# A transformer block's attention: where the score products stand among the four heads' transposed scores

## The chip, the cores and the metric

The kernel runs on one core of a Trainium2 chip. The metric is the time of one execution on the device in microseconds, as a median of several runs.

## What is computed

One transformer block with adaptive modulation, in fp32, on x of 2 batch rows x 2048 tokens x 512 channels, 16 heads of 32 channels, a hidden layer of 2048:

```python
mod = jax.nn.silu(condition) @ Wada + bada
sh_a, sc_a, gt_a, sh_m, sc_m, gt_m = jnp.split(mod, 6, axis=1)
xm = layernorm(x, g1, be1) * (1.0 + sc_a[:, None, :]) + sh_a[:, None, :]
x = x + gt_a[:, None, :] * attention(xm, Wqkv, Wproj, bproj)
xm = layernorm(x, g2, be2) * (1.0 + sc_m[:, None, :]) + sh_m[:, None, :]
h = gelu(xm @ W1 + b1)
return x + gt_m[:, None, :] * (h @ W2 + b2)
```

The attention is causal: scores q k^T * 32**-0.5, a softmax over the keys up to the query's own place, then times v.

## The kernel before

**Stages.** For each batch row: layer norm, modulation and the q, k, v products (class Qkv), then attention (attention_phase), then the output projection (project_phase). The feed-forward part follows for both rows at the end. q and k are split into a high and a low part of 32 channels each, which stand side by side, so that one product with 128 contraction rows gives a head's full score.

**Units and steps.** Attention of one row is cut into 16 units: four groups of four heads (c), each with four blocks of 512 queries (i), in the order of the list units. A unit goes through its keys in steps of one tile of 128 keys (steps_of, line 631), with the last three diagonal tiles in two steps. A step (scores_t, line 524) makes the *transposed scores* of the four heads, keys down and queries across: first four selector products (line 550: sel with fold) that put minus the query's maximum into each head's st bank, then for every head the product of keys and queries on top of it (line 558). ScalarE takes the exponential of each head's bank into a tile e (line 566); GpSimd masks it on the diagonal (line 572) and adds pairs of e (line 592). Two steps later (LAG) the value products (o from e and vv, line 606) and the row sums (sm) follow.

**Score products.** The maxima that a unit needs have to be known before its own steps begin. They come from plain scores, queries down and keys across: Row.bank (line 422) makes one product of up to 512 keys in a PSUM bank, and VectorE reduces it to a maximum (lines 436 and 441, mx). Row.split (line 444) makes the high and low part of a unit's maxima, Row.rows (line 492) spreads them into fold. These score products are put among the steps of the units ahead. How many a step gets is planned: every product has a cost (line 267), every step a weight and a due time (due, line 644), and row.count (line 460) gives n for the step. Row.score(n, borrow) (line 470) issues n products; each takes one of two s banks, or, where borrow is given, every other one a bank of the ring of four st banks. A step issues more than five before its selectors (line 545). Up to five remain: those of head h follow it if h >= HC - n (line 579), and a fifth comes at the end (line 581). The one behind head 2 is the *borrowed* score product.

**Banks.** PSUM has two s banks, four st banks, one o and one sm. The st ring is taken in order: four heads, then the borrowed product, which gets the bank that the step's head 0 had; the next step's four heads get those of heads 1, 2, 3 and the borrowed one. A bank is free when its reader, ScalarE's exponential or VectorE's reduction, is through.

**Order.** Matmuls, exponentials, masks and sums are kept in program order (mm, line 190, and act, line 194); an instruction that waits holds up those behind it on its engine. The last unit has no score products left.

Of the kernel before, what the change touches and what calls it, by code (L numbers as in the profile page):

```python
# [27 lines left out]
def dit_block_kernel(  # L28
# [41 lines left out]
    HC = P // HD  # L70
# [119 lines left out]
    def mm(*args, **kw):  # L190

        return tc.keep_in_program_order(nc.tensor.matmul(*args, **kw))  # L192

    def act(ins):

        return tc.keep_in_program_order(ins)
# [318 lines left out]
    def attention_phase(row):  # L515
        b, vv, kst, qst = row.b, row.vv, row.kst, row.qst
        with pool(f"att{b}") as ap, pool(
# [6 lines left out]
            def scores_t(u, step, n):  # L524

                def st_bank():

                    n_bank[0] += u == len(units) - 1
                    if n_bank[0] % 6 > HC:
                        return ps_sp.tile([P, QB], F32, tag="s", name="st")
                    return ps_stp.tile([P, QB], F32, tag="st", name="st")

                c, i = units[u]  # L540
                tiles = steps_of[u][step]
                q0 = tiles[0][1]
                w = sum(QB - q for _, q in tiles)
                sts, es = [], []
                row.score(max(0, n - 5))
                n = min(n, 5)
                for h in range(HC):
                    g = slice(h * HD, (h + 1) * HD)
                    st = st_bank()
                    mm(  # L550
                        st[:, :w], sel[g, :], fold[u % 2][g, q0 : q0 + w],
                        start=True, stop=False,
                    )
                    sts.append(st)
                for h in range(HC):
                    at = 0
                    for j, q in tiles:
                        mm(
                            sts[h][:, at : at + QB - q],
                            kst[c][:, h, j * P : (j + 1) * P],  # L560
                            qst[u][:, h, q:],
                            start=False, stop=at + QB - q == w,
                        )
                        at += QB - q
                    e = ap.tile([P, QB], F32, tag="e", name="e", bufs=E_BUFS)
                    act(nc.scalar.activation(e[:, :w], sts[h][:, :w], AF.Exp))  # L566
                    if tiles[0][0] >= i * TQ:

                        d = e.rearrange("p (t k) -> p t k", k=P)[:, 0 : TQ : TQ - 1, :]
                        d = d[:, : len(tiles), :]  # L570
                        act(
                            nc.gpsimd.affine_select(  # L572
                                d, d, pattern=[[0, len(tiles)], [1, P]],
                                compare_op=ALU.is_ge, fill=0.0,
                                base=0, channel_multiplier=-1,
                            )
                        )
                    es.append(e)
                    if h >= HC - n:
                        row.score(1, st_bank if h == 2 else None)  # L580
                row.score(n - HC)
                return es

            def new_sums():
# [59 lines left out]
            def due(u, step):  # L644

                rate, past = 0.0, weight[step]
                for v in range(u + 1, len(units)):

                    left = sum(weight[step : max(step + 1, starts[v] - 3)])
                    rate = max(rate, (cum[v] - row.spent) / left)  # L650
                return row.spent + rate * past

            for u, (c, i) in enumerate(units):
# [5 lines left out]
                for n_step, tiles in enumerate(steps_of[u]):  # L659
                    last = n_step == steps - 1  # L660
                    if n_step == 0:
# [4 lines left out]
                    n = row.count(  # L666
                        due(u, starts[u] + n_step) - QB // 2, u + AHEAD
                    )
                    es = scores_t(u, n_step, n)
                    make_rows = False  # L670
                    if u + 1 < len(units) and row.rows_made == u + 1:
# [300 lines left out]
    row = Row(0)  # L972
# [115 lines left out]
    first, row = row, Row(1)  # L1088
# [31 lines left out]
    with ExitStack() as mlp:  # L1120
# [249 lines left out]
        for m in range(NM):  # L1370
            h = [
                [
                    mp.tile([P, 4, MT], F32, tag="h4", name="h4", bufs=2 * FC // 4)
                    for _ in range(FC // 4)
                ]
                for _ in range(2)
            ]
# [87 lines left out]
```

## Time and profile before

| what | value |
|---|---|
| median of 3 runs | 2526.72 us (2524.92 to 2527.82) |
| profiled execution, its own time | 2526.39 us |
| its span in the profile | 2524.7 us |
| granted TensorE clock, mean | 0.99 |
| attention of row 0 | about 225 to 760 us of the span |
| attention of row 1 | about 1100 to 1653 us of the span |
| score products in all (s and borrowed) | 1058 + 222 |
| mean VectorE reduction of a 128x512 bank (L441) | 686 ns |
| mean exponential of one head (L566) | 576 ns |

Names: PE is TensorE's matmuls, PEld its weight loads, DVE VectorE, ACT ScalarE, POOL GpSimd, SPq SyncE's queue of transfers. A row of the timeline gives the start and the length in us, the engine, the line of the kernel, the operation, the tiles out<-in, the sizes, how many alike follow each other (x4), and in brackets the idle time before it and what ended that. A row of the groups view gives the same with a count, the busy time and the mean in ns, and the idle time ahead of the group with what ended most of it. A row of waits names an engine and tile, whom it waited for, total us, times and the longest. Nearly all matmuls carry line 192, that of a helper, so they are told apart by tiles: `s<-kst,qst` is a score product in an s bank, `st<-kst,qst` a borrowed one, `st<-qst,kst` a head's transposed scores, `st<-fold,sel` a selector product.

### The profile page before, as it was taken

To read this page: it belongs to the slowest core of one execution; us is meant where nothing else is said; L and a number is where in the kernel's file an instruction comes from. 1 tells how busy PE (TensorE), PEld (TensorE's weight loads), DVE (VectorE), ACT (ScalarE), POOL (GpSimd) and SP (SyncE) were. 2 spreads that over 40 slices of the span, in tenths; PEclk is the share of its full clock that TensorE was granted. 3 is DMA by queue.
4 is the path that set the end of the run, shared out by engine and by line. 5 is a ranking of instruction groups with operands and counts; after the bars stand their busy time and mean duration, and the time that the engine had idled before them with its cause. 6 is when DMAs were issued, how large, how long until landed. Compare 5 with 4: busy or idle time off the path is not lost.

```text
span 2524.7 us, 30931 instructions
## 1 busy us (share of the span) xinstructions
PE 2460.4 (97%) x10977; PEld 1172.8 (46%) x10977; DVE 1351.5 (54%) x2820; ACT 895.1 (35%) x1667; POOL 982.0 (39%) x1158
## 2 busy tenths in 40 slices
PE   7999999999999899999999999999999999999998
PEld 3445445444444344554444444444444444444443
DVE  3465657667565625656675756665353353344424
ACT  2213455454545011155545454613312312311310
POOL 0062786766772362058767785241101201200200
PEclk9999999999999999999999999999999999999999
DMA  6667123041224596450514113163223233322422
GB/s 221 208 223 193 39 52 84 22 109 43 87 90 141 193 296 200 133 109 22 109 43 93 39 38 134 68 219 119 87 92 132 85 100 108 108 93 72 140 84 96
DMA packets 133445, 285.71 MB, mean 113 GB/s; under 512 B 13301, under 2 KB 42525, under 8 KB 128426
## 3 DMA queue, kind: packets, MB, share of 16 engines
q1 hardware_dynamic: 126226, 257.47, 34.2%
q0 software_dynamic: 5376, 23.07, 2.6%
q10 hardware_dynamic: 1688, 3.19, 0.4%
q8 instruction: 86, 1.41, 0.2%
q14 instruction: 69, 0.57, 0.1%
HBM read 209.76 MB, written 81.79 MB: 115 GB/s over the span
## 4 chain that ended last, share of the span: by engine, by line
PE 61%; DVE 2%; DMA 1%; SPq 1%; issue 0%; ACT 0%; POOL 0%; DVEq 0%; ACTq 0%
PE ps_y L192 15%; PE ps_h L192 15%; PE st L192 9%; PE o L192 5%; PE s L192 4%; PE ps_qk L192 4%; PE ps_o L192 2%; PE sm L192 2%; PE ps_v L192 2%; SPq L336 1%; PE ps_xt L200 1%; DVE junk L436 1%; PE ps_o L200 0%; DVE mx L441 0%; DMA r<-sum 0%
## 5 line engine op out<-in xcount | busy, mean ns | idle before, releaser
L566 ACT ACTIVATE e<-st 128x512 f32<-128x512 f32 (+1 forms) x1152 | 575.3, 576 | 509.4 <-PE st L192 460.5
L441 DVE TENSOR_REDUCE mx<-s 128x1 f32<-128x512 f32 x616 | 413.7, 686 | 273.5 <-PE s L192 272.1
L592 POOL TENSOR_TENSOR ee<-e 128x512 f32<-128x512 f32 x336 | 420.9, 1287 | 246.3 <-ACT e L566 245.7
L192 PE MATMUL s<-kst,qst 128*128 128x512 f32 (+3 forms) x1058 | 453.5, 447 | 17.8 <-DVE mx L436 8.5
L192 PE MATMUL st<-qst,kst 128*128 128x512 f32 (+3 forms) x1280 | 438.1, 392 | 0.0
L192 PE MATMUL o<-e,vv 128*32 128x512 f32 (+3 forms) x2560 | 294.9, 542 | 0.0
L192 PE MATMUL ps_h<-sx,w 128*128 128x512 f32 x640 | 286.7, 592 | 0.0
L436 DVE CUSTOM_DVE_ANT_0 junk<-s,causal 128x384 bf16<-128x384 f32 (+3 forms) x442 | 211.1, 478 | 138.9 <-PE s L192 130.6
L1236 POOL TENSOR_TENSOR c<-c 128x512 f32<-128x512 f32 x32 | 40.6, 1270 | 620.9 <-DVE c L1198 620.9
L192 PE MATMUL ps_y<-sh,w 128*128 128x512 f32 x640 | 277.5, 593 | 0.0
L192 PEld LDWEIGHTS st<-qst,kst 128*128 128x128 f32 x1280 | 230.4, 192 | 88.0 <-issue 63.3
L192 PEld LDWEIGHTS s<-kst,qst 128*128 128x128 f32 x1058 | 199.3, 190 | 144.0 <-issue 47.7
L192 PE MATMUL ps_qk<-xmT,wqkv 128*128 128x512 f32 x512 | 242.3, 601 | 2.2 <-DVE xmT L248 2.2
L572 POOL TENSOR_SCALAR_AFFINE_SELECT e<-e 128x128 f32<-128x128 f32 (+1 forms) x384 | 124.3, 341 | 289.3 <-ACT e L566 282.8
L1198 DVE TENSOR_TENSOR h<-c,ps_h 128x512 f32<-128x512 f32 x128 | 88.0, 687 | 232.5 <-PE ps_h L192 232.5
L592 POOL TENSOR_TENSOR ee<-ee 128x512 f32<-128x512 f32 x168 | 210.8, 1283 | 0.0
L192 PEld LDWEIGHTS ps_h<-sx,w 128*128 128x128 f32 x640 | 121.1, 190 | 150.2 <-issue 149.5
L192 PEld LDWEIGHTS ps_y<-sh,w 128*128 128x128 f32 x640 | 121.1, 191 | 148.3 <-issue 146.9
L192 PE MATMUL st<-fold,sel 32*128 32x512 f32 (+1 forms) x1152 | 156.8, 485 | 2.7 <-DVE fold L500 2.0
L1222 ACT ACTIVATE h<-h,cols 128x512 f32<-128x512 f32 x128 | 92.3, 721 | 182.0 <-DVE h L1198 182.0
L192 PEld LDWEIGHTS st<-fold,sel 32*128 32x128 f32 x1152 | 62.2, 183 | 183.8 <-ACT e L566 124.8
L192 PEld LDWEIGHTS ps_qk<-xmT,wqkv 128*128 128x128 f32 x512 | 95.2, 192 | 98.9 <-issue 91.8
(124 smaller groups left out, 2368.9 us busy)
## 6 DMA issues: line engine op xcount, KB each, us to landing
qst<-q SPq DMA_DIRECT2D x128, 256.0 KB
w<-w1d SPq DMA_DIRECT2D x34, 896.0 KB
w<-w2d SPq DMA_DIRECT2D x28, 1024.0 KB
kst<-k SPq DMA_DIRECT2D x24, 1024.0 KB
q<-hl SPq DMA_DIRECT2D x32, 512.0 KB
k<-hl SPq DMA_DIRECT2D x32, 512.0 KB
kst<-k SPq DMA_DIRECT2D x32, 256.0 KB
w<-in_L_cond_W_dram POOLq DMA_DIRECT2D x64, 128.0 KB, 4.7
```

The costliest lines, as they stand in the source:

```text
L192: return tc.keep_in_program_order(nc.tensor.matmul(*args, **kw))
L200: return tc.keep_in_program_order(nc.tensor.transpose(dst, src, ident[:n, :n]))
L336: nc.sync.dma_start(dst, inv_d[self.b][u].unsqueeze(1).to_broadcast([HC, HD, QB]),)
L436: nc.vector.tensor_tensor_reduce(junk[:, :w], s[:, :w], causal[:, QB - w :], 1.0, MASKED, ALU.add, ALU.max, m,)
L441: nc.vector.tensor_reduce(m, s[:, :w], axis=AX.X, op=ALU.max)
L566: act(nc.scalar.activation(e[:, :w], sts[h][:, :w], AF.Exp))
L572: nc.gpsimd.affine_select(d, d, pattern=[[0, len(tiles)], [1, P]], compare_op=ALU.is_ge, fill=0.0, base=0, channel_multiplier=-1,)
L592: act(engine.tensor_tensor(dst, x, y, ALU.add))
L1198: nc.vector.tensor_tensor(dst, x, y, op)
L1222: nc.scalar.activation(d, d, AF.Gelu, bias=col(r_b1 + chunk, 1))
L1236: nc.gpsimd.tensor_tensor(c1_, c1_, c2_, ALU.subtract)
```

## The change

In a step with n of three or more score products (after the cap at five), one follows head 0 and one follows head 1, both in s banks; the third is borrowed and stands behind head 3; the others follow it, in s banks. In a step with fewer than three they stand as before, behind the last heads, and none is borrowed. The list of score products, their number in each step, the sizes and all other work are the same.

```diff
                     es.append(e)
-                    if h >= HC - n:
-                        row.score(1, st_bank if h == 2 else None)
-                row.score(n - HC)
+                    if h < 2 and n >= 3 or h >= HC - n and n < 3:
+                        row.score(1)
+                if n >= 3:
+                    row.score(1, st_bank)
+                    row.score(n - 3)
                 return es
```

## Prediction

> **What bounds the kernel now.** I read the page first, then the costliest groups, then the timeline of single steps. The page shows TensorE busy nearly throughout, so a gain has to be a hole between TensorE's products or an interval in which its next weights are not in.
>
> ```profile
> PE 2460.4 (97%) x10977; PEld 1172.8 (46%) x10977; DVE 1351.5 (54%) x2820; ACT 895.1 (35%) x1667; POOL 982.0 (39%) x1158
> ```
>
> The groups view says where TensorE's weight loads wait. The borrowed score products (tile st, but operands kst and qst exchanged) number 222, and their loads wait for ScalarE almost alone; the other score products wait for VectorE.
>
> ```profile
> L192 PEld LDWEIGHTS s<-kst,qst 128*128 128x128 f32 x1058 | 199.3, 190 | 144.0 <-issue 47.7 <-DVE mx L441 47.3 <-DVE mx L436 20.9
> L192 PEld LDWEIGHTS st<-kst,qst 128*128 128x128 f32 x222 | 41.8, 188 | 57.7 <-ACT e L566 56.0
> ```
>
> The timeline of a step with four score products shows what such a wait costs. First the weight loads, then the matmuls:
>
> ```profile
> 618.89 0.19 PEld L192 LDWEIGHTS st<-qst,kst 128*128 128x128 f32 x1
> 619.34 0.19 PEld L192 LDWEIGHTS st<-kst,qst 128*128 128x128 f32 x1 [0.26 <-ACT e L566]
> 619.45 0.19 PEld L192 LDWEIGHTS st<-qst,kst 128*128 128x128 f32 x1
> ```
> ```profile
> 619.12 0.40 PE L192 MATMUL st<-qst,kst 128*128 128x512 f32 x1
> 619.35 0.49 PE L192 MATMUL st<-kst,qst 128*128 128x512 f32 x1
> 619.68 0.39 PE L192 MATMUL st<-qst,kst 128*128 128x512 f32 x1
> 619.91 0.40 PE L192 MATMUL s<-kst,qst 128*128 128x512 f32 x1
> 621.23 0.50 PE L192 MATMUL st<-fold,sel 32*128 32x512 f32 x4
> ```
>
> 512-wide products follow each other in 0.23 us. The borrowed one holds its bank until ScalarE has finished the first head's exponential. Its load comes at 619.34 instead of 619.12, so it no longer lies under the product before it, and the next product starts 0.33 us later: 0.10 us lost. ScalarE's row gives the release: four exponentials from 618.69, each 576 ns, so the first ends at 619.27.
>
> ```profile
> 618.69 2.07 ACT L566 ACTIVATE e<-st 128x512 f32<-128x512 f32 x4 [0.43 <-PE st L192]
> ```
>
> With five score products the last of them can wait as well, for VectorE to read the second of the two s banks (0.34 us idle here):
>
> ```profile
> 630.20 0.19 PEld L192 LDWEIGHTS st<-kst,qst 128*128 128x128 f32 x1 [0.27 <-ACT e L566]
> ...
> 631.08 0.19 PEld L192 LDWEIGHTS s<-kst,qst 128*128 128x128 f32 x1 [0.34 <-DVE mx L441]
> ```
>
> With two, the borrowed product follows three heads directly and TensorE stands still:
>
> ```profile
> 648.64 0.96 PE L192 MATMUL st<-qst,kst 128*128 128x512 f32 x3
> 649.89 0.50 PE L192 MATMUL st<-kst,qst 128*128 128x512 f32 x1 [0.29 <-ACT e L566]
> ```
>
> [...] loads normally start with the product before (0.23 us apart), and a waiting borrowed product holds up the fourth head's product behind it. [...] I count distances between successive products, not idle time. [...] the 128x16 cast takes 0.17 us at best and up to 1.27 us between 500 and 760 us.
>
> **The change part by part.** *Which steps.* Working through the planner's costs and due times gives per batch row 54 steps with 5 products, 26 with 4, 23 with 6, 3 with 7, 4 with 2 and one with 3; doubled, 222, as in the groups. The timeline shows the same number in every step. Nothing of the counts, the order in which score products are taken, or other engines' work changes.
>
> *Four and more products (212 steps).* Order now: head 0, s, head 1, s, head 2, borrowed, head 3, s, s. After: head 0, s, head 1, s, head 2, head 3, borrowed, s, s. Only the borrowed product and head 3 change places. The borrowed one is due 0.23 us later, and waits for the same exponential. Its loss here was 0.08 to 0.25 us in nearly every step, larger where a narrow product ahead shortens the way, so the shift covers nearly all of it: bound 0 to (old loss less 0.23), I take 0. What is late next is the last score product: its s bank is free only when VectorE has read the product two before it, and that moment does not move. So I rebuilt the end of every step from the timeline: the borrowed product without loss, each last score product at the later of its own pace and (observed end of that reduction + 0.06 us to the load + 0.50 us to its end, narrower ones less).
>
> *Three (2 steps).* Both plain products go first, the borrowed one last: loss 0.33 each gone. *Two (8 steps).* No borrowing any more; both products use s banks, behind heads 2 and 3, that VectorE has long read. Loss 0.56 each gone; bound 0 to a VectorE wait of some 0.3 us, I take 0.
>
> Sums over both rows, in us (products in the step: steps, loss at the borrowed product, of it kept at the step's end):
> 2: 8, 4.5, 4.5. 3: 2, 0.7, 0.7. 4: 52, 6.2, 4.8. 5: 108, 15.8, 3.8. 6 and 7: 52, 7.2, 1.5. Together 34.4, of which 15.2 (before rounding) is kept; three steps that lie in a stretch of lowered clock are set at nothing kept. Of the 108 steps with five products, 78 keep nothing: their last score product waits for VectorE anyway.
>
> *To be taken off.* (a) After six of the eight two-product steps ScalarE is late: fourth exponential done 0.10 + 2.08 + 0.06 us after head 0's product, selector load wanted at 5 x 0.23 + 0.93 = 2.08 (0.93 from the end of the last score product, 620.30, to that load, 621.23, in the first step shown): 0.16 each, 1.0 together. (b) In the fourteenth unit VectorE waits for a load of the sums, which SyncE issues behind ten slow transfers:
>
> ```profile
> 689.77 20.54 SPq L336 DMA_DIRECT2D wide<-inv  x10
> 710.36 2.41 SPq L322 DMA_DIRECT2D r<-sum  x1
> ```
> ```profile
> 721.59 0.25 DVE L329 RECIPROCAL r<-r 128x16 f32<-128x16 f32 x1 [4.54 <-DMA r<-sum]
> ```
>
> What eight steps gain ahead of it is waited away: 0.45 per row, 0.9. (c) Steps that end sooner leave VectorE less time to catch up: bound 0 to 3, I take 0.5. The sum: 15.2 - 1.0 - 0.9 - 0.5 = 12.8 us.
>
> *New queue.* The borrowed product's wait now has the last one or two s products and the value products behind it instead of head 3. Head 3's product ends up to 0.43 us sooner, which gives ScalarE nothing: it is still at the earlier heads (four in 2.07 us). VectorE gets the borrowed product 0.03 (loss was 0.2) to 0.13 us later (loss was 0.1), while it is usually still on the second product. The next step's fourth selector product needs that bank: in the step above, read at 620.07 + 0.69 = 620.76, wanted at 621.23, so 0.4 us of slack.
>
> The profiled execution took 2526.4 us, the median is 2526.7. 2526.4 - 12.8 = **2513.6 us**.
>
> **Rivals.** (1) VectorE paces every step with four or more products: not only the waits seen but the slack elsewhere is used up. For it: VectorE waits of 47.3 + 20.9 us stand ahead of score loads. Against: in 40 of the 52 four-product steps no such wait follows. Left: 4.5 + 0.7 - 1.0 = 4.2, so 2522.2 us. (2) Slower: the borrowed product reaches VectorE 0.13 us later in the 89 steps whose loss was near 0.1, VectorE runs dry, and the delay reaches TensorE through the fourth head's bank or the next step's s bank. It decides once VectorE is 0.4 us later than shown. If two such delays a step stick, 2 x 89 x 0.13 = 23, less 4.2: 2545 us; half of it, 2534. Against: VectorE works without a gap from the second product into the borrowed one in the step shown. (3) More: collisions of VectorE with GpSimd at the splits fall otherwise. At 594 to 598 us one makes two score products wait 1.10 and 0.52 us; four such places, two per row: up to 6 us more, 2507.5.
>
> **How the numbers follow.** About 0.2% (5 us) is what a measurement of this kernel can tell from no change. Forecast as worked, 2508 to 2519: 0.75. Rival 1, 2519 to 2525: 0.13. Rival 2: 0.05. Rival 3, below 2508: 0.07. Faster: 0.75 + 0.07 + 0.01 of rival 1's lower part = 0.83; same 0.12; slower 0.05. The range, 2507 to 2520, takes in (c) at 0 and at 3, the first sum without any deduction (2511.2), a part of rivals 1 and 3, and leaves out less than 2 in 10.
>
> **What would show it.** In the changed kernel 214 borrowed products, and nearly none of the 56 us of waiting for ScalarE ahead of their loads; more than 68 us of waiting for VectorE ahead of s loads; four-product steps shorter by 0.1 to 0.2 us, wide five-product steps as long as before, the two-product steps before units' ends shorter by 0.5 us. It is wrong if borrowed loads still wait, if selector loads wait for VectorE, or if the four-product steps keep their length.

## The result, and the profile after

| | before | after |
|---|---|---|
| median, us | 2528.39 (2524.21 to 2530.41, 10 runs) | 2519.30 (2513.87 to 2529.32, 10 runs) |
| profiled execution, its own time | 2526.39 | 2519.99 |
| its span | 2524.7 | 2518.3 |

The ratio is 0.9967 (95% interval 0.9952 to 0.9982), a gain of 9.1 us by the medians where 12.8 was forecast; the interval allows 4.6 to 12.1. The forecast of 2513.6 us lies below every one of the runs, of which the best took 2513.87. The direction was right, the size was not.

The page and the groups view of the kernel after, in the same form as those shown of before:

```profile
PE 2445.9 (97%) x10977; PEld 1181.8 (47%) x10977; DVE 1412.4 (56%) x2820; ACT 891.6 (35%) x1667; POOL 981.3 (39%) x1158
```
```profile
L192 PEld LDWEIGHTS s<-kst,qst 128*128 128x128 f32 x1066 | 201.5, 189 | 168.6 <-DVE mx L441 68.1 <-issue 47.4 <-DVE mx L436 26.4
L192 PEld LDWEIGHTS st<-kst,qst 128*128 128x128 f32 x214 | 40.5, 189 | 16.1 <-ACT e L566 0.8
```

There are 214 borrowed products, and of 56.0 us of waiting for ScalarE 0.8 are left. The s loads wait 94.5 us for VectorE instead of 68.2. One number doesn't fit a change of order only: VectorE has the same 2820 instructions, but is busy for 1412.4 us instead of 1351.5.

The end of a step with four products, matmuls on the timeline:

```profile
613.77 0.63 PE L192 MATMUL st<-qst,kst 128*128 128x512 f32 x2
614.24 0.39 PE L192 MATMUL st<-kst,qst 128*128 128x512 f32 x1
614.47 0.40 PE L192 MATMUL s<-kst,qst 128*128 128x512 f32 x1
```

The heads' last two, the borrowed product and the s product follow each other in 0.23 us. In a step with five the wait has moved to the load of the last product:

```profile
625.48 0.19 PEld L192 LDWEIGHTS s<-kst,qst 128*128 128x128 f32 x1 [0.42 <-DVE mx L441]
```

And in a step with two, where 0.29 us of idle time stood before the product behind the third head, it follows at once:

```profile
642.70 0.96 PE L192 MATMUL st<-qst,kst 128*128 128x512 f32 x3
643.50 0.39 PE L192 MATMUL s<-kst,qst 128*128 128x512 f32 x1
```

**Where the rest went.** The time from each step's first head product to the next step's, called the step's length here, says where the loss is. Only three of the 288 steps are longer in the kernel after by more than 0.2 us, if those are left aside in which the clock fell (below): the first step of the ninth and thirteenth units of row 0 and of the fifth unit of row 1, by 1.86, 1.13 and 3.21 us, of the last 1.7 by the clock. A load in the first of them, in the kernel after:

```profile
512.58 0.19 PEld L192 LDWEIGHTS s<-kst,qst 128*128 128x128 f32 x1 [2.04 <-DVE mx L441]
```

VectorE reads that bank late since it was standing at the cast of Row.split (line 455), 128x16 elements. Such an instruction is called held below, and the time that it takes a hold:

```profile
497.00 14.68 DVE L455 CAST mhl<-m 128x16 fp32r<-128x16 f32 x1
...
511.85 0.68 DVE L441 TENSOR_REDUCE mx<-s 128x1 f32<-128x512 f32 x1
```

GpSimd works without a gap over these 14.7 us:

```profile
494.24 10.00 POOL L594 TENSOR_TENSOR ee<-e 128x512 f32<-128x512 f32 x8
504.14 1.10 POOL L572 TENSOR_SCALAR_AFFINE_SELECT e<-e 128x128 f32<-128x128 f32 x4
505.16 2.56 POOL L594 TENSOR_TENSOR ee<-ee 128x512 f32<-128x512 f32 x2
507.62 1.54 POOL L572 TENSOR_SCALAR_AFFINE_SELECT e<-e 128x256 f32<-128x256 f32 x4
509.07 2.57 POOL L594 TENSOR_TENSOR ee<-ee 128x512 f32<-128x512 f32 x2
```

The same place in the kernel before, VectorE and GpSimd:

```profile
503.70 1.27 DVE L455 CAST mhl<-m 128x16 fp32r<-128x16 f32 x1
```
```profile
499.93 5.01 POOL L592 TENSOR_TENSOR ee<-e 128x512 f32<-128x512 f32 x4
505.18 4.99 POOL L592 TENSOR_TENSOR ee<-e 128x512 f32<-128x512 f32 x4 [0.24 <-ACT e L566]
```

There GpSimd ran out of exponentials for 0.24 us at 504.94, and the cast ended at 504.97. In the kernel before all six splits of this kind, those of the sixth, tenth and fourteenth units of either row, end their cast within 0.04 us of the start of such a gap, of 0.24 to 0.71 us. After the change TensorE and ScalarE are further ahead at this place: the exponential that GpSimd had to wait for is done 0.7 us before GpSimd comes to it, and the gap is gone, here and at the other five. The tile view gives a cast's minimum, median and maximum in ns, first for after, then for before; with the subtractions (line 456, up to 6573 ns against 1210) the sum over both is 89.5 us against 30.3, which is 59.2 of the 60.9 us that VectorE is busier.

```profile
L455 DVE CAST mhl<-m x24: 164/776/14695, 166.8 to 1587.6; 128x16 fp32r<-128x16 f32 x24
```
```profile
L455 DVE CAST mhl<-m x24: 165/810/1270, 166.7 to 1594.6; 128x16 fp32r<-128x16 f32 x24
```

**The clock.** A second thing has to be taken out before steps are compared. In the fourteenth unit TensorE waits behind the load of the sums, in row 0 of the kernel after for 4.62 us without a product, and its granted clock falls to 0.50 for some microseconds, which is called a dip here. The stretches show it (columns: stretch, its length, busy time of PE, granted clock, DMA share, GB/s), again of the kernel after:

```profile
715.00:717.00 2.00, 0.00 (x0) 0.85 0.28 112
717.00:719.00 2.00, 1.70 (x6) 0.50 0.16 49
719.00:721.00 2.00, 2.00 (x8) 0.50 0.10 28
721.00:723.00 2.00, 2.00 (x14) 0.50 0.25 94
723.00:725.00 2.00, 2.00 (x12) 0.94 0.02 9
```

A stretch is counted as losing its length times (1 - clock). Eight value products show what it stands for: 1.94 us at 720.15, with the clock at 0.50, and 1.06 at 724.62, with 1.00. Here the loss is 2 x (0.15 + 0.50 + 0.50 + 0.50 + 0.06) = 3.4 us; at the same place of the kernel before, with clocks of 0.80, 0.50 and 0.85 in three such stretches, 2 x (0.20 + 0.50 + 0.15) = 1.7. All dips in the thirteen profiles of this study, but for those that the end of the span cuts off, cost close to 1.7 us, or two or three times as much; in the kernels before and after they last 3.41, 6.83 or 10.24 us at a clock of 0.50. They agree in place too: in each profile's record of the clock they start whole multiples of the shortest one's length apart (in the kernel before, those at 449.13 and 722.20 us, by 273.07 us, which is 80 times 3.413), and counted back from a dip to the start of the span, whole lengths leave another remainder in each (1.98 us in the kernel before, 3.02 in the one after). That one kernel's execution can gain or lose 1.7 or 3.4 us at a place without any cause in its code is inferred from this and not shown, since each kernel was profiled once. Below, a ledger is the sum of the differences of step lengths between two profiles, by the number of score products in the step. It has the clock's part taken out of every step, as the sum of (1 - clock) over half-microsecond stretches.

### The profile page after: what moved, and what is told of

It is laid out like the page before. It is cut to its first block, busy times and chain, and to the rows that moved or that the text cites. A ratio compares the mean times of both kernels' runs of the same rounds, so it can differ in the third digit from the quotient of the medians.

```text
span 2518.3 us, 30927 instructions
## 1 busy us (share of the span) xinstructions
PE 2445.9 (97%) x10977; PEld 1181.8 (47%) x10977; DVE 1412.4 (56%) x2820; ACT 891.6 (35%) x1667; POOL 981.3 (39%) x1158
## 4 chain that ended last, share of the span: by engine, by line
PE 86%; DVE 8%; DMA 3%; SPq 2%; issue 1%; ACT 1%; POOL 0%; DVEq 0%; ACTq 0%; POOLq 0%
PE st L192 16%; PE ps_y L192 15%; PE ps_h L192 15%; PE o L192 9%; PE ps_qk L192 8%; PE s L192 8%; PE sm L192 4%; PE ps_v L192 4%; PE ps_o L192 3%; DVE mx L441 2%; DVE mhl L455 2%; SPq L336 2%; DMA r<-sum 1%; DVE junk L436 1%; PE ps_xt L200 1%
## 5 line engine op out<-in xcount | busy, mean ns | idle before, releaser
L192 PE MATMUL s<-kst,qst 128*128 128x512 f32 (+3 forms) x1066 | 468.7, 454 | 29.3 <-DVE mx L441 15.4
L192 PE MATMUL st<-qst,kst 128*128 128x512 f32 (+3 forms) x1280 | 403.5, 391 | 0.0
L436 DVE CUSTOM_DVE_ANT_0 junk<-s,causal 128x256 bf16<-128x256 f32 (+3 forms) x444 | 211.9, 477 | 132.4 <-PE s L192 123.9
L192 PEld LDWEIGHTS st<-qst,kst 128*128 128x128 f32 x1280 | 224.2, 191 | 92.8 <-issue 63.2
```

The costliest lines, as they stand in the source:

```text
L436: nc.vector.tensor_tensor_reduce(junk[:, :w], s[:, :w], causal[:, QB - w :], 1.0, MASKED, ALU.add, ALU.max, m,)
```

## The experiments

Times are compared with runs of the kernel before on the same chip. After that comes what the ledger of the steps says.

### One part at a time

Only the part for three and more products:

```diff
-                    if h < 2 and n >= 3 or h >= HC - n and n < 3:
+                    if h < 2 and n >= 3:
                         row.score(1)
+                    elif h >= HC - n and n < 3:
+                        row.score(1, st_bank if h == 2 else None)
```

> Only the part of the change for three or more score products; steps with two borrow behind head 2 as before. Theory A (the missing gain is a hold: VectorE's 128x16 split of the maxima finds no gap in GpSimd's run of sums and masks, and first score products of units 5, 9 and 13 wait for it): the borrowed products keep their gain, some 10 us against the kernel before; whether the hold is there depends on whether GpSimd still has its 0.24 us gap near the end of units 4, 8 and 12. With gaps: casts of at most 1.3 us and 9 to 11 us faster than before; without: casts of 7 to 15 us and 3 to 5 us faster. Rival B (VectorE's reductions alone pace the steps, the casts cost nothing): 5 to 6 us faster than before whatever the casts take.

Measured: 2519.02 us (2515.53 to 2520.47, 5 runs) against 2527.09 (12 runs), ratio 0.9963 (0.9951 to 0.9976). Steps with four products gain 4.6 us over both rows, with five 4.3, with three 0.7. The long casts are there: 14.1 us in the tenth split of row 0 and the sixth of row 1, where the next unit's first step loses 1.1 and 1.4 us (in row 0 a dip of the clock adds 1.7), and 7.0 and 6.8 us at two others, where nothing is lost. In the last place of either row GpSimd still has a gap of 0.24 and 0.20 us, and the casts take 1.28 and 1.33.

Only the part for two products:

```diff
-                    if h < 2 and n >= 3 or h >= HC - n and n < 3:
-                        row.score(1)
-                if n >= 3:
-                    row.score(1, st_bank)
-                    row.score(n - 3)
+                    if h >= HC - n:
+                        row.score(1, st_bank if h == 2 and n >= 3 else None)
+                row.score(n - HC)
```

> Only the part for fewer than three: eight steps lose their borrowed product, all others as in the kernel before. Theory A: each of the eight steps is shorter by 0.41 to 0.56 us, 3.7 us in all, but in six of them the maxima of a unit are completed, so the split comes early into GpSimd's run: casts of several us appear, the first score products of units 5, 9 and 13 wait 1 to 3 us in some places, and the total is between 3.7 us faster and 3 us slower than before. Rival B: 3.7 us faster, no long cast.

Measured: 2523.01 us (2518.87 to 2530.82, 8 runs), ratio 0.9983 (0.9970 to 0.9997). The eight steps gain 3.7 us. No cast takes more than 1.39 us, so the expectation of long casts fell, and its rival B, 3.7 us and no long cast, came true. But that is not because GpSimd kept its gaps. At four of the six places it has none, and VectorE still gets in, with the cast at the end of one of GpSimd's additions (502.14 us here) and with the subtraction at the end of the next (503.39):

```profile
501.59 0.59 DVE L455 CAST mhl<-m 128x16 fp32r<-128x16 f32 x1
502.21 1.22 DVE L456 TENSOR_TENSOR mhl<-m,mhl 128x16 fp32r<-128x16 f32 x1
```
```profile
500.85 7.48 POOL L592 TENSOR_TENSOR ee<-e 128x512 f32<-128x512 f32 x6
```

So a gap always ended a hold, and a missing gap did not always make a long one. In the six profiles of this study that leave these splits, or their subtraction alone, on VectorE, ten of the 36 places have a gap, and their holds take at most 1.4 us; 26 have none, of which 22 hold VectorE for 6.8 us or more and these four for 1.8 us with both instructions. By the medians the two parts of the change gain 8.1 and 4.1 us by themselves, and only 9.1 together.

### The split away from VectorE

Both instructions of the split on GpSimd, in program order with its sums; once in the kernel after, once in the kernel before:

```diff
-            nc.vector.tensor_copy(hl[:, :, :, 0], m)
-            nc.vector.tensor_tensor(
-                hl[:, :, :, 1], m, hl[:, :, :, 0].bitcast(F32), ALU.subtract
-            )
+            act(nc.gpsimd.tensor_copy(hl[:, :, :, 0], m))
+            act(
+                nc.gpsimd.tensor_tensor(
+                    hl[:, :, :, 1], m, hl[:, :, :, 0].bitcast(F32), ALU.subtract
+                )
+            )
```

> The changed kernel with the two small operations of the split (128x16 cast and subtraction) on GpSimd instead of VectorE. Theory A: no VectorE instruction stands held, the 6.2 us of waits at the first steps of units 5, 9 and 13 go, and the four places in units 7 and 11 where two score products wait 1.0 and 0.5 us go too: 8 to 12 us faster than the changed kernel, 17 to 21 faster than the kernel before, and the runs lie closer together. Rival B: within 2 us of the changed kernel, since the reductions stay as they are. Rival C (GpSimd is itself the late engine): GpSimd's longer queue delays masks and sums, value products wait, 2 to 6 us slower than the changed kernel.

> The kernel before with the same two operations on GpSimd. Theory A: the holds of the kernel before are short (at most 1.3 us) and reach TensorE only at the four places in units 7 and 11, 1.6 us each: 4 to 7 us faster than before. The difference between this and the changed kernel with the same edit is then the change alone, 12 to 14 us. Rival B: no change against before, and 9 us between the two edited kernels.

Measured: 2506.22 us (2505.61 to 2507.11, 4 runs; ratio 0.9915, 0.9901 to 0.9928) and 2518.01 us (2515.61 to 2523.62, 5 runs; ratio 0.9964, 0.9950 to 0.9978). Between these two the change is worth 11.8 us instead of 9.1. GpSimd's timeline in the changed kernel with this edit:

```profile
498.69 0.21 POOL L455 CAST mhl<-m 128x16 fp32r<-128x16 f32 x1
498.99 0.22 POOL L457 TENSOR_TENSOR mhl<-m,mhl 128x16 fp32r<-128x16 f32 x1
```

The split now stands between two sums and takes 0.5 us, and the load that had waited 2.04 us waits 0.17, at 510.19. The first steps of the three units gain 1.9, 1.1 and 3.2 us, of the last 1.7 by the clock. But both kernels also gain elsewhere, 6.4 and (apart from the clock) 6.0 us: the fifth steps of the seventh and eleventh units of each row, where cast and subtraction had taken 0.9 and 1.2 us, are some 1.5 us shorter. So the split on VectorE costs at these places too, with or without the change.

Only the cast away, to ScalarE, in the kernel after; the subtraction stays:

```diff
-            nc.vector.tensor_copy(hl[:, :, :, 0], m)
+            act(nc.scalar.copy(hl[:, :, :, 0], m))
```

> The changed kernel with the cast alone on ScalarE; the subtraction, which reads two operands in SBUF, stays on VectorE. If any VectorE operation [...] is held, the hold moves to the subtraction: instructions of 6 to 15 us there, and the time within 3 us of the changed kernel. If only the cast [...] is held, the holds are gone: 8 to 12 us faster than the changed kernel.

Measured: 2506.63 us (2505.63 to 2508.94, 6 runs), ratio 0.9919 (0.9906 to 0.9932). The hold moved to the next VectorE instruction of the split. Its cast takes 0.2 us on ScalarE, and VectorE's timeline at the worst place is

```profile
1480.62 13.97 DVE L456 TENSOR_TENSOR mhl<-m,mhl 128x16 fp32r<-128x16 f32 x1 [0.27 <-ACT mhl L455]
```

Yet the time is that of the kernel with both instructions moved. In the ledger the fifth steps of the seventh and eleventh units gain 5.3 us, the ninth unit's first step of row 0 1.9, the clock 1.7, while the thirteenth unit's of row 1 loses 1.1; with all small terms attention gains 8.8 of the 12.7 us between the medians. So most of what this kernel gains within attention comes from the seventh and eleventh units, not from the long holds. The two profiles differ by 14.0 us: 5.2, of them 1.5 by the clock, lie outside attention, and 3.6 of these behind the start of row 1's last step, where nothing was edited. That stretch differs anyway from profile to profile: it takes from 876.3 us, here, to 879.8, in the kernel after.

### The three long holds alone, and the others alone

The next three kernels move the split to GpSimd only in some units of each row: the sixth, tenth and fourteenth, where the holds were long, in the kernel after and in the kernel before; and in the kernel after only the eighth, twelfth and sixteenth (`u in (7, 11, 15)`):

```diff
+            if u in (5, 9, 13):
+                act(nc.gpsimd.tensor_copy(hl[:, :, :, 0], m))
+                act(
+                    nc.gpsimd.tensor_tensor(
+                        hl[:, :, :, 1], m, hl[:, :, :, 0].bitcast(F32), ALU.subtract
+                    )
+                )
+                return
             nc.vector.tensor_copy(hl[:, :, :, 0], m)
```

> The changed kernel with the split on GpSimd in only three units of each row, those whose cast or subtraction VectorE was held at for 7 to 15 us (the sixth, tenth and fourteenth). Theory (the hold of these splits ate a part of the gain): the losses of 6.2 us at the first score products of the ninth and thirteenth units are gone, about 2513 us, and its runs lie within some 4 us instead of 15, since the holds that hang on a fraction of a microsecond are gone; the steps before the eighth and twelfth units stay as in the changed kernel. Rival (what moving all splits gave was VectorE's time in general): three of sixteen splits give three sixteenths of 13 us, about 2517 us, with the same spread as before.

> The kernel before with the same three splits of each row on GpSimd. Theory: there the casts took 1.3 us at most and made nobody wait, so 2526.5 to 2528.5, within 0.1% of the kernel before; the change alone is then 14 to 15 us between this and its counterpart. Rival (moving these splits helps whatever the order): several us below the kernel before, and the change alone stays at 9 to 10 us.

> The changed kernel with the split on GpSimd in the eighth, twelfth and sixteenth unit of each row only, where the cast took 0.9 to 1.0 us and the subtraction 1.2. Theory: the waits there, which the kernel before has too, are gone, about 7 us, 2512 us; the long holds at the other splits stay, with the first score products of the ninth and thirteenth units as late as in the changed kernel, and the runs spread over 10 us or more. Rival (the long holds are what all of the 13 us hang on): within 2 us of the changed kernel.

Measured: 2515.15 us (2510.39 to 2517.24, 6 runs; ratio 0.9956, 0.9943 to 0.9970), 2527.21 us (2521.40 to 2530.54, 14 runs; ratio 1.0003, 0.9994 to 1.0012) and 2507.23 us (2504.24 to 2509.20, 5 runs; ratio 0.9927, 0.9914 to 0.9941), against 2526.15 (19 runs).

The first two are the cleanest pair. In the kernel before, moving these splits gains nothing; in the kernel after, the three first steps gain exactly 1.87, 1.14 and 3.21 us. Between the medians of the two lie 12.1 us, where the change alone had given 9.1. The total of the kernel after gained less than its three steps, 4.5 us between the profiles, since in the profile of this kernel the clock fell at two places where it had not in the profile of after, in the seventh unit of each row. Stretches of one of them:

```profile
446.00:447.00 1.00, 0.77 (x6) 0.59 0.00 0
...
452.00:453.00 1.00, 1.00 (x8) 0.50 0.00 0
453.00:454.00 1.00, 1.00 (x11) 1.00 0.00 0
```

Both follow the fifth step there, in which TensorE's loads wait for VectorE four times behind the split, 0.4 to 1.2 us each. The kernels that leave the whole of the eighth and twelfth splits on VectorE have 24 such places in their six profiles, and five of them are followed by a dip that costs 3.4 us; the kernels that don't have 28 in seven, and none is.

The third kernel was 5 us faster than the better of its two expectations, and taught most. It leaves the sixth, tenth and fourteenth splits on VectorE, they are still held, and still the first steps lose nothing:

```profile
496.24 7.33 DVE L463 CAST mhl<-m 128x16 fp32r<-128x16 f32 x1
...
509.20 0.69 DVE L441 TENSOR_REDUCE mx<-s 128x1 f32<-128x512 f32 x1 [5.38 <-PE s L192]
```

The hold ends after 7.33 us, when VectorE has 5.4 us to spare until the next score product; the one of 14.68 us ran past it. That holds without exception in the profiles of these kernels: after 14 us (14.68, 14.70 and 7.62 + 6.57 in the kernel after, 14.1 twice in the first experiment, 14.02, 14.68 and 13.97 with the cast on ScalarE) the next unit's first step is 1.1 to 1.9 us longer, apart from the clock; after 7 us (6.8 to 7.6, in the same kernels and in this one) it isn't. On its side this kernel has a new hold: the cast of the ninth and thirteenth splits, 0.17 us before, takes 2.6 to 2.7 in both rows, score products come right behind it, and the first steps of the eighth and twelfth units lose 1.1 to 1.2 us each. What counts is not the hold's length but whether a score product falls due in it.

### The wait in the fourteenth unit

The inverse of the last sums two steps later in that unit, with the spreading of its result right behind it, so that VectorE doesn't wait for the transfer; on top of the split on GpSimd, in both kernels:

```diff
-            elif n == 4:
+            elif n == (6 if u == n_early + 1 else 4):
                 self.invert(u - 1, u)
-            elif n == 5:
+                if u == n_early + 1:
+                    self.widen(u - 1)
+            elif n == 5 and u != n_early + 1:
                 self.widen(u - 1)
```

> The changed kernel with the split on GpSimd (2506.2 us) and, in the fourteenth unit, the reciprocal of the last sums two steps later, so that VectorE doesn't stand waiting for the load of the sums. Theory A with the prediction's deduction (b): the wait of 5.4 us per row in the fourteenth unit goes or shrinks to about 1 us, and with it the stretch of lowered TensorE clock behind it: 6 to 11 us faster than with the split on GpSimd alone, 2496 to 2500 us. Rival: the wait only moves to the first step of the fifteenth unit, less than 2 us faster.

> The kernel before with both of these edits, without the change. Theory A: the change alone, between this kernel and the changed one with the same edits, is worth 13 to 15 us (11.8 us with the wait in the fourteenth unit still there, which swallowed or lengthened 1 to 3 us): 2509 to 2515 us. Rival (nothing was swallowed there): 11 to 12 us between the two.

Measured: 2491.06 us (2488.51 to 2492.53, 4 runs; ratio 0.9855, 0.9839 to 0.9871) and 2507.63 us (2505.66 to 2508.87, 6 runs; ratio 0.9920, 0.9906 to 0.9934). The first is the best version of all, 36 us below the kernel before. Against the same kernel without this edit the tenth step of that unit is shorter by 6.6 us in row 0 and by 6.3 in row 1, of which 3.2 and 2.9 are the clock: TensorE no longer stands there, and the dip doesn't come (a stretch of the same view, with TensorE busy throughout and the clock at 1.00):

```profile
712.00:716.00 4.00, 4.00 (x29) 1.00 0.07 14
```

Between these two the change alone is worth 16.6 us.

### A second borrowed product

In steps with five products the last one borrowed as well, on top of the split on GpSimd in the kernel after:

```diff
-                    row.score(1, st_bank)
-                    row.score(n - 3)
+                    row.score(n - 2, st_bank)
```

> The changed kernel with the split on GpSimd, and in steps with five score products the fifth borrowed as well, so that the last one doesn't wait for VectorE to read the second s bank. If banks are what limits the five-product steps, they become 0.2 to 0.4 us shorter in 78 of 108 cases: 15 to 30 us faster than with the split alone. If VectorE's reductions pace them (rival 1 of the prediction, for these steps alone), the wait moves to the selector products of the next step, which need the bank: within 5 us of it either way.

Measured: 2516.55 us (2516.06 to 2519.88, 6 runs), ratio 0.9959 (0.9946 to 0.9972): 10 us slower than without, twice what I had allowed. The waits view of this kernel has a new row (in us, times, longest):

```profile
PEld s L192 <- DVE mx L441: 30.5, 47, 3.3
PEld st L192 <- DVE mx L441: 12.9, 39, 0.5
```

Without the edit the first row was 63.1 us, and the second was not there. The fifth product no longer waits for an s bank; the next step's selectors wait (the row with st), since a bank that they take is one that VectorE has not read.

Steps with five products lose 9.5 us, those with six 3.8. So another bank doesn't help: at the end of such a step VectorE's reading sets the pace, which is the prediction's reason why 78 of the 108 wide steps keep nothing. That the loss is so large because a selector that waits holds up all heads behind it is argued from the program order, not shown. Nor is VectorE short of time in the whole step: in the kernel after it is busy for 71% of the steps with five products, and stands idle before their first score product arrives, 1.0 us in the median. Whether an earlier first product would help was not tried.

## Why the prediction was right in kind and wrong in size

The ledger of attention, in us over both rows, next to the terms of the forecast (with (a), the late exponential, taken from the row of two). The columns are the change by itself, the same with the split on GpSimd throughout, and with it there in three units:

| products in the step | forecast | before to after | split on GpSimd | three splits on GpSimd |
|---|---|---|---|---|
| 2, less (a) | 3.5 | 3.7 | 3.7 | 3.7 |
| 3 | 0.7 | 0.7 | 0.7 | 0.7 |
| 4 | 4.8 | 4.5 | 4.5 | 4.5 |
| 5 | 3.8 | 4.4 | 4.3 | 4.4 |
| 6 | 1.5 with 7 | 0.8 | 1.1 | 1.2 |
| 7 | | -4.5 | 0.0 | 0.0 |
| none | 0 | -0.1 | -0.9 | -0.6 |
| clock | 0 | 0.0 | 0.0 | 0.0 |
| sum | 14.3, less (b) and (c) 12.8 | 9.4 | 13.3 | 13.8 |

**The terms that held.** The losses at the borrowed products, and what is kept of them: 14.3 us were forecast for them before (b) and (c), and 14.0, 14.2 and 14.4 came out (before rounding) if the steps with seven and with none are left aside. That the sums are so close is in part luck, since steps with four gained 0.3 less than forecast, those with five 0.6 more and those with six 0.7 less. The late exponential (a) is right: two-product steps after which ScalarE is late gain 0.41 to 0.44 us, the two others 0.56. "What is late next is the last score product" is right; its wait is in the timeline, and with the second borrowed product it moved to the next bank that VectorE had to read.

**The step that failed.** The working had no term for Row.split. Its instructions were in it only as rival (3), with a sign: collisions with GpSimd "fall otherwise, up to 6 us more". They did fall otherwise, and took 4.5 us of waiting at three places, and 1.7 us of clock at one of them. The sign was taken from the places between 594 and 598 us, where the split costs in the kernel before and could only improve. Those hardly changed: cast and subtraction took 1.01 and 1.20 us there before, 0.94 and 1.20 after. The loss came at splits that had cost nothing: 1.27 us was read there as the price of a collision, while it was the time up to GpSimd's next gap. The change took the gap away, and VectorE was held for 7 or 14 us; with these three splits of each row on GpSimd the 4.5 us are back. By the prediction's own sum: the kept terms came out at 14.0 instead of 12.8 net, 4.5 go for the missing term and 0.1 in steps without products, which leaves the 9.4 of the ledger. The clock's parts cancel in this pair: +3.4 in the seventh unit of row 0, where only before had a dip, +1.7 at the start of row 1's attention, -1.7 in the fifth unit of row 1, -1.7 in either fourteenth unit. The two profiled executions differ by only 6.4 us; outside attention the dips cost 1.4 us more after than before, and 1.6 us lie elsewhere. (In the kernel before the first and last products of attention stand at 225 and 805 us in row 0, at 1074 and 1651 us in row 1; 760 and 1100 in the table of the kernel before are wrong.)

**Term (b).** 0.9 us were to be swallowed by the wait for the sums. TensorE's wait there grew from 4.15 to 4.82 us in row 0 and from 3.96 to 4.48 in row 1: 1.2 together. With the wait gone in both kernels, the steps with six products gain 1.9 us instead of 1.1, which is 0.8, and the five rows together 15.2. Mechanism and size are right. What the prediction didn't see is the dip that follows the wait, 1.7 us in each row before and 3.4 after. That those are longer in the kernel after is not due to the change as far as the runs show: with the split on GpSimd it is 3.4 and 1.7 in the kernel before, 3.4 and 3.4 in the one after, and with three splits there 1.7 and 3.4, 1.7 and 1.7.

**Term (c).** VectorE's lost time for catching up, 0.5 us: nothing in the ledgers needs it. Steps with four products gain 0.3 less than worked out, those with five 0.6 more.

**Rivals.** (1), VectorE paces every step with four products: no, those steps gain 4.5 us. (2), the borrowed product comes late and VectorE runs dry: no; the selector loads wait for VectorE no longer than before (3.1 us for fold in both), and no step but the three named is longer by more than 0.2 us, those with a dip of the clock aside.

**The spread.** The changed kernel's ten runs lie 15.5 us apart, the four of the version with the split on GpSimd 1.5. A part of it is the clock: the mean granted clock, which is on record for every run, was 0.985 in the slowest of the ten and 0.989 in the fastest, and 0.004 of 2520 us is 10 us, an estimate, since it is recorded to three digits. That holds are drawn anew in each execution as well would fit the rest, but only one execution of each kernel was profiled: argued, not shown.

**What stays open.** What decides whether a hold without a gap ends with the GpSimd instruction under way, as with the two-product steps alone, or after 7 or 14 us. The long ones that I read end within 0.2 us of a change of GpSimd from sums to masks (503.4 us for the 7.33, 511.53 for the 14.68, 1494.47 for the 13.97), but the long one passed two such changes, at 504.14 and 507.62. And what makes the work outside attention take some us more or less from profile to profile, as with the cast on ScalarE.

## What to carry to other kernels

Where a short instruction takes far longer than its work, as a cast of 0.17 us did here, its recorded length tells when the hold ended, not what it costs: here 1.3 us with a gap of GpSimd, and without one anything from 0.6 to 14.7. Before a change that makes a pipeline run more evenly, look for the gaps at which such holds end, here within 0.04 us at six places: what got better was that GpSimd's input, an exponential, came in time, by 0.7 us, and that took away its gap. Then ask what falls due behind the instruction: here only a hold into which a score product fell cost time, 1.1 to 1.9 us for those of 14 us. Where TensorE stands for some microseconds, price the clock that falls behind it as well, here 1.7 or 3.4 us after stands of 2.2 to 4.6, and take it out before two executions are compared step by step.

## What was not expected of the hardware

- A VectorE cast or subtraction of 128x16 elements, 0.17 us by itself, was held for up to 14.7 us, over some eighteen GpSimd instructions of 0.3 to 1.3 us that followed each other directly. The trace shows the hold, and not what VectorE waited for. Not every VectorE instruction was held: a reduction of 128x512 from PSUM at 495.43 us and one of 128x48 from SBUF at 496.76 took their usual 0.69 and 0.20 us while the same GpSimd run went on.
- The same split on GpSimd takes 0.20 + 0.22 us, on VectorE 0.17 + 0.17 when nothing holds it, and still the changed kernel is faster with it on GpSimd, by 13 us.
- A dip of the granted clock to 0.50 costs 1.7 us or two or three times that, and followed each of the 22 stands in the fourteenth unit (2.2 to 4.6 us) in the eleven profiles that have them; the two without have no dip there.
